# Two-layer FFN in half-size products: separate PSUM banks with vector sums, or shared PSUM banks with ScalarE copies of partial sums

## The chip, the cores and the metric

The kernel runs on one core of a Trainium2 chip. A core has five engines with a queue of instructions each, worked off strictly in the order of the queue: TensorE (PE; its weight loads are listed apart as PEld) for matrix products, VectorE (DVE), ScalarE (ACT) and GpSimd (POOL) for elementwise work, and SyncE (SP), which here issues most DMAs. An instruction that waits for a semaphore holds up everything behind it on its engine. The matrix engine writes its results into PSUM, eight banks of 512 float32 columns on 128 partitions; all other tiles are in SBUF.

The metric is the device time of a whole execution in microseconds, as a median of several. Beside it stands one profiled execution with a trace of every instruction.

## What is computed

Eight batches of 1024 rows of 256 numbers go through an attention block without learned projections and then through a two-layer FFN, both with adaptive layer norm and gates that come from a small vector per batch. All of it is float32.

```python
x = L0_attn_x                                    # (8, 1024, 256)
mod = (silu(L0_c) @ L0_wmod).reshape(8, 6, 1, -1)
sa, ca, ga, sb, cb, gb = (mod[:, n] for n in range(6))
ga, gb = gates pushed away from zero (at least 0.25 in size)
h = layernorm(x) * (1 + ca) + sa
scores = einsum('nsd,ntd->nst', h * w_lhs, h * w_rhs)
x = x + ga * einsum('nst,ntd->nsd', softmax(scores), h)
h = layernorm(x) * (1 + cb) + sb
y = relu(h @ W1 + b1) @ W2 + b2                  # 256 -> 1024 -> 256
out = x + gb * y
```

## The kernel before

A batch is cut into eight row tiles of 128 rows (`i` = 0 to 7), and its FFN into two groups of 512 rows (`g` = 0, 1). The main loop runs over batches `b` and tiles `i`. A step (b, i) computes the scores of the tile two ahead (`direct`, tile `psc`, L412), copies them to SBUF on ACT (L419), mirrors the symmetric part by a DVE transpose and two DMAs (`mirror`, L435, `move`, L306 and L309), turns the row maximum on PE (`max_turn`, tile `pm`, L468), subtracts it on DVE (L475), takes the exponent on ACT (`exponent`, L484; `weights` does both), and multiplies an earlier tile with the values (`product`, tile `po`, L501). Tiles 1 and 2, 3 and 4, 6 and 7 are multiplied in pairs, with seven half-size products in the place of eight (`pair_begin`, L549, tile `pp`; `pair_end`, L593, tiles `pq`, `pr`; their left-hand sums `left_sums` on POOL; `pair_out` on DVE).

Between these stands the FFN of the batch before (`fb = b - 1`): group 0 in steps 0 to 3, group 1 in steps 4 to 7. Both of its layers use the same scheme of seven half-size products with sums before and after. In the first layer a *pair* is chunk `c` and chunk `c + 4` of the eight chunks of 128 hidden units, over the two halves of the 512 rows (`lo`, `hi`, 256 columns). The products of a pair go to three PSUM banks `pa`, `pb`, `pc`; `pa` is copied to SBUF by ACT (`kept`, L747), and its first half is used again by the seventh product (`pair_last`). DVE forms the result `f` in five sums (`pair_sums` and L779), POOL adds the last term (L780), ACT applies the relu (`pair_relu`, L789 and L790), and POOL forms the four differences that the second layer needs (`pair_turn`, L799 to L802). Two pairs stand in each of the steps 0, 1, 4 and 5. The second layer runs in steps 2 and 3, and 6 and 7 (`y_first`, `y_second`, L806, tiles `ya`, `yb`, `yc`, `yd`), with seven sums on DVE and a scaling with the gate on ACT (`y_gate`, L857). The result is transposed on DVE (`y_turn`), sent through DRAM and back, and added to `x` on POOL (`y_add`, L880).

Steps also prepare the next batch: statistics on DVE (L241), 1/std on ACT (`prepare_rstd`, L247 and L248), the normalised rows `xg` on ACT (`prepare_norm`, L281, with a small shift `rs` from DVE, L277), their transpose on DVE and through DRAM (`prepare_blocks`, tiles `T_a` and `X_a`, L322), and from it the two sides of the score product on ACT (`prepare_turn_apart`, L342, tiles `rT`, `lT`). `spare` takes small POOL operations from a queue. The last batch's FFN stands after the loop, with a direct second layer (`second`, L916).

Every engine's order is the order in which the code calls these functions; `pin` holds the scheduler to it. PSUM is three pools: two banks for scores (tag `s`), two for transposes and maxima (tag `t`), four for everything else (tag `a`).

Of the kernel before, what the change touches and what calls it, by code (L numbers as in the profile page):

```python
# [17 lines left out]
P = 128  # L18
# [6 lines left out]
def adaln_block_kernel(  # L25
# [30 lines left out]
    ps_s = ctx.enter_context(tc.tile_pool(name="ps_s", bufs=2, space=PSUM))  # L56
    ps_t = ctx.enter_context(tc.tile_pool(name="ps_t", bufs=2, space=PSUM))
    ps_a = ctx.enter_context(tc.tile_pool(name="ps_a", bufs=4, space=PSUM))
    dram = ctx.enter_context(tc.tile_pool(name="dram", bufs=1, space=bass.MemoryType.DRAM))

# [79 lines left out]
    def warm(n):  # L140

        pw = ps_s.tile([P, HALF], F32, tag="s", name=f"pw_{n}")
        nc.tensor.matmul(pw[:, :n], lhsT=zeros[:, :P], rhs=zeros[:, :n], start=True, stop=True)
# [12 lines left out]
    pt_c = ps_t.tile([P, HALF], F32, tag="t", name="pt_c")  # L156
# [18 lines left out]
    def columns(src, at):  # L175
        n = src.shape[0]
        pv = ps_t.tile([P, HALF], F32, tag="t", name=f"pt_v{at}")
        nc.tensor.transpose(pv[:, :n], src, ident[:n, :n])
        nc.scalar.copy(cols[:, ds(at, n)], pv[:, :n])
# [9 lines left out]
    def mod_rows(part, parts):  # L189

        pm = ps_a.tile([P, HALF], F32, tag="a", name=f"pmr_{part}")
        w = parts * D
        for k in range(ND):
            nc.tensor.matmul(  # L194
                pm[:B, :w],
                lhsT=scT[:, k, :],
                rhs=wm[:, k, ds(part * D, w)],
                start=(k == 0),
                stop=(k == ND - 1),
            )  # L200
        nc.scalar.copy(
            mod[:, part : part + parts, :].rearrange("b s d -> b (s d)"), pm[:B, :w]
        )

    def mod_columns(part):

        pc = ps_a.tile([P, HALF], F32, tag="a", name=f"pmc_{part}")
# [140 lines left out]
    def prepare_turn(b, g, vector=True):  # L348
# [5 lines left out]
        for k in range(ND):  # L354
            if b > 0:
                pt = pre[b, g][:, k]
            else:
                pt = ps_t.tile([P, HALF], F32, tag="t", name=f"pth_{b}_{g}_{k}")
# [44 lines left out]
    def direct(b, i, parts=range(S // HALF)):  # L403
        if i == 0 and parts[0] == 0:
            sc_t[b] = two.tile([P, NT, NV, NT, V], F32, tag="sc", name=f"sc_{b}", bufs=1)
        for n in parts:
# [3 lines left out]
            psc = ps_s.tile([P, HALF], F32, tag="s", name=f"psc_{b}_{i}_{n}")  # L410
# [33 lines left out]
    def mirror_first(i):  # L444
        sc = first_scores()
        j = i + 1
        while j < NT:
            n = min(TH, NT - j)
            pool, tag = (ps_t, "t") if j == i + 1 else (ps_a, "a")
            pt = pool.tile([P, HALF], F32, tag=tag, name=f"ptm_{i}_{j}")  # L450
# [15 lines left out]
    def max_turn(b, i):  # L466
        pm = ps_t.tile([P, HALF], F32, tag="t", name=f"pm_{b}_{i}")
# [25 lines left out]
    def product(b, i, parts=(0, 1)):  # L493
        pT = pT_t[b, i]
        if 0 in parts:
            po_t[b, i] = ps_a.tile([P, HALF], F32, tag="a", name=f"po_{b}_{i}")
# [42 lines left out]
    def pair_begin(b, i, between=None):  # L539

        W = work.tile([P, 2, D + 4], F32, tag="W", name=f"W_{b}_{i}", bufs=1)
        pp = ps_a.tile([P, HALF], F32, tag="a", name=f"pp_{b}_{i}")
# [36 lines left out]
    def pair_end(b, i):  # L579
# [3 lines left out]
        pq = ps_a.tile([P, HALF], F32, tag="a", name=f"pq_{b}_{i}")  # L583
        pr = ps_a.tile([P, HALF], F32, tag="a", name=f"pr_{b}_{i}")
        for out, lhs, rhs in (
# [5 lines left out]
        ):  # L591
# [95 lines left out]
    def ffn_turn(b, g):  # L687
        hT = two.tile([P, ND, HALF], F32, tag="hT", name=f"hT_{b}_{g}", bufs=1)
        split = lambda T: T.rearrange("p (t a v) -> p t a v", a=NV, v=V)
        if (b, g) == (0, 0):  # L690
            xn, X = ffn.pop(("xn", g))[0], []
            for k in range(ND):
                pt = ps_t.tile([P, HALF], F32, tag="t", name=f"ptx_{b}_{g}_{k}")
# [29 lines left out]
    pairs = {}  # L723

    def mm(out, lhsT, rhs):
        nc.tensor.matmul(out, lhsT=lhsT, rhs=rhs, start=True, stop=True)  # L726

    def pair_products(b, g, c, between=None):
# [6 lines left out]
        n = ts(c, P)  # L735
        s1, a22 = (w1[:, k, ds((c + NH) * P, P)] for k in range(2))

        pool, tag = (ps_s, "s") if b == B - 1 else (ps_a, "a")
        pa = ps_a.tile([P, HALF], F32, tag="a", name=f"pa_{b}_{g}_{c}")
        pb = pool.tile([P, HALF], F32, tag=tag, name=f"pb_{b}_{g}_{c}")  # L740
        pc = ps_a.tile([P, HALF], F32, tag="a", name=f"pc_{b}_{g}_{c}")
        mm(pa[:, lo], w1[:, 0, n], hT[:, 0, lo])
        mm(pa[:, hi], s1, hs[:, 0])

        tag, bufs = ("s1", 1) if b == B - 1 and c % 3 == 2 else ("kept", 2)
        kept = work.tile([P, HALF], F32, tag=tag, name=f"kept_{b}_{g}_{c}", bufs=bufs)
        nc.scalar.copy(kept, pa)  # L747
        mm(pb[:, lo], w1s[:, 0, n], hs[:, 1])
        mm(pb[:, hi], w1s[:, 1, n], hs[:, 2])
        mm(pc[:, lo], w1[:, 1, n], hT[:, 1, lo])  # L750
        mm(pc[:, hi], a22, hT[:, 0, hi])
        if between:
            between()
        pairs[c] = pa, pb, pc, kept

    def pair_sums(b, g, c):
        pa, pb, pc, kept = pairs[c]
        f = ffn["f"]
        u = work.tile([P, H2], F32, tag="u", name=f"u_{b}_{g}_{c}", bufs=2)
        pairs[c] = pa, kept, u  # L760
        far = f[:, c + NH, hi]
        nc.vector.scalar_tensor_tensor(
            u, pb[:, lo], b1_col(c), kept[:, lo], ALU.add, ALU.add
        )
        nc.vector.scalar_tensor_tensor(  # L765
            far, pb[:, hi], b1_step[:, c : c + 1], u, ALU.add, ALU.add
        )
        nc.vector.scalar_tensor_tensor(
            f[:, c, lo], pc[:, lo], b1_col(c), kept[:, lo], ALU.add, ALU.add
        )  # L770
        nc.vector.tensor_tensor(f[:, c + NH, lo], pc[:, hi], far, ALU.add)

    def pair_last(b, g, c):


        pa, kept, u = pairs.pop(c)
        f = ffn["f"]
        mm(pa[:, lo], w1s[:, 2, ts(c, P)], ffn["hT", g][0][:, 1, hi])
        nc.vector.tensor_tensor(f[:, c, hi], pa[:, lo], u, ALU.add)  # L779
        nc.gpsimd.tensor_tensor(  # L780
            f[:, c::NH, hi],
            f[:, c::NH, hi],
            kept[:, None, hi].to_broadcast([P, 2, H2]),
            ALU.add,
        )

    def pair_relu(c):
        f = ffn["f"]
        nc.scalar.activation(f[:, c, :], f[:, c, :], AF.Relu)  # L789
        nc.scalar.activation(f[:, c + NH, :], f[:, c + NH, :], AF.Relu)  # L790

    def pair_turn(c):


        f, ft = ffn["f"], ffn["ft"]
        add = nc.gpsimd.tensor_tensor
        add(ft[:, 0, c], f[:, c + NH, hi], f[:, c, hi], ALU.subtract)  # L799
        add(ft[:, 1, c], ft[:, 0, c], f[:, c, lo], ALU.add)  # L800
        add(ft[:, 2, c], ft[:, 1, c], f[:, c + NH, lo], ALU.subtract)
        add(f[:, c, hi], f[:, c, hi], f[:, c, lo], ALU.subtract)  # L802

    def over_pairs(out, lhs, rhs):
        for c in range(NH):
            nc.tensor.matmul(  # L806
                out, lhsT=lhs(c), rhs=rhs(c), start=(c == 0), stop=(c == NH - 1)
            )

    def y_first(b, g, between=None):  # L810

        Y = ffn["Y"] = two.tile([P, 2, HALF], F32, tag="Y", name=f"Y_{b}_{g}", bufs=1)
        f, ft = ffn["f"], ffn["ft"]
        ya = ps_a.tile([P, HALF], F32, tag="a", name=f"ya_{b}_{g}")
        yb = ps_a.tile([P, HALF], F32, tag="a", name=f"yb_{b}_{g}")
        over_pairs(ya[:, lo], lambda c: w2[:, c, 0:P], lambda c: f[:, c, lo])
        over_pairs(yb[:, lo], lambda c: w2[:, c + NH, 0:P], lambda c: f[:, c + NH, lo])
        nc.scalar.copy(Y[:, 0, lo], ya[:, lo])
        if between:
            between()  # L820
        over_pairs(ya[:, hi], lambda c: w2s[:, 1, c], lambda c: ft[:, 1, c])
        over_pairs(yb[:, hi], lambda c: w2[:, c, P:D], lambda c: ft[:, 0, c])
        ffn["y"] = ya, yb

    def y_first_sums():
        Y, (ya, yb) = ffn["Y"], ffn.pop("y")
        add = nc.vector.tensor_tensor
        add(Y[:, 1, hi], ya[:, hi], Y[:, 0, lo], ALU.add)
        add(Y[:, 0, lo], yb[:, lo], Y[:, 0, lo], ALU.add)
        add(Y[:, 1, lo], yb[:, hi], Y[:, 1, hi], ALU.add)  # L830

    def y_second(b, g, between=None):

        f, ft = ffn["f"], ffn["ft"]
        yc = ps_a.tile([P, HALF], F32, tag="a", name=f"yc_{b}_{g}")
        yd = ps_a.tile([P, HALF], F32, tag="a", name=f"yd_{b}_{g}")
        over_pairs(yc[:, lo], lambda c: w2s[:, 0, c], lambda c: f[:, c, hi])
        if between:
            between()
        over_pairs(yc[:, hi], lambda c: w2s[:, 2, c], lambda c: f[:, c + NH, hi])  # L840
        over_pairs(yd[:, lo], lambda c: w2[:, c + NH, P:D], lambda c: ft[:, 2, c])
        ffn["y"] = yc, yd

    def y_second_sums(b):

        Y, (yc, yd) = ffn["Y"], ffn.pop("y")
        add = nc.vector.tensor_tensor
        add(Y[:, 0, hi], yc[:, lo], Y[:, 1, hi], ALU.add)
        add(Y[:, 1, hi], yc[:, lo], Y[:, 1, lo], ALU.add)
        add(Y[:, 0, hi], yc[:, hi], Y[:, 0, hi], ALU.add)  # L850
        add(Y[:, 1, lo], Y[:, 1, lo], yd[:, lo], ALU.subtract)

    def y_gate(b):

        Y = ffn["Y"]
        for h in range(2):
            nc.scalar.activation(  # L857
                Y[:, h], Y[:, h], AF.Identity,
# [593 lines left out]
```

## Time and profile before

| | us |
|---|---|
| two runs | 757.01, 758.22 (median 757.62) |
| profiled execution, first to last instruction | 755.1 |
| one batch in the middle (b = 3, at 258 to 349 us) | about 90.5 |
| busy DVE / ACT / POOL | 574.9 / 374.9 / 570.9 |
| granted TensorE clock | 1.000 |

Mean durations of what is added, removed or moved, from the groups of the page (form: output tile):

| line, engine, operation | ns | count |
|---|---|---|
| L747 ACT copy `kept<-pa` 128x512 | 584 | 64 |
| L789 ACT relu `f` 128x512 | 622 | 64 |
| L484 ACT exponent `pT` 128x1024 | 1056 | 64 |
| L818 ACT copy `Y<-ya` 128x256 | 384 | 14 |
| L762, L765, L768 DVE sum of three 128x256 | 475 to 484 | 64 each |
| L771, L779 DVE sum of two 128x256 | 414, 404 | 64 each |
| L780 POOL sum 128x512 | 1274 | 64 |
| L799 to L802 POOL difference 128x256 | 727 to 729 | 56 each |
| L475 DVE subtract 128x1024 | 1208 | 64 |

In a timeline row the first number is the start in us from the beginning of the span, the second the time from that start to the end of the last of the merged instructions. A matrix instruction in float32 appears as two records, each with a modelled end that overlaps the next start; the distance between starts is what TensorE takes. A bracket at a row's end tells how long the engine stood idle before it and which operation it then waited for.

### The profile page before, as it was taken

Reading aid. Unit: us, or ns where it says so; the run is one execution under the profiler, and the core shown is the slowest. Engines: PE = TensorE matmul, PEld = TensorE weight load, DVE = VectorE, ACT = ScalarE, POOL = GpSimd, SP = SyncE. Lnnn points to the kernel's source line nnn. Section 1 sums busy time; section 2 is a strip of 40 time slices with the busy share of each in tenths; the row PEclk is TensorE's granted clock in tenths of the full one; section 3 lists DMA queues with packets and bytes.
Section 4 is the critical chain, followed back from the end, with each engine's and each line's share of the span. In section 5 each row is a group of like instructions: output and inputs, shape, how many; then the busy total and the mean of one; then the engine's idle time right before and its main releaser. Section 6 shows DMA issues by size and latency. Waiting matters only on the chain.

```text
span 755.1 us, 11883 instructions
## 1 busy us (share of the span) xinstructions
PE 749.1 (99%) x3876; PEld 623.4 (83%) x3876; DVE 574.9 (76%) x1259; ACT 374.9 (50%) x688; POOL 570.9 (76%) x658
## 2 busy tenths in 40 slices
PE   8999999999999999999999999999999999999998
PEld 4686889788897888888888878988889788888887
DVE  7787879778796879968878688876889777685632
ACT  4554646635375454745546444563546535252521
POOL 3762796878968798788877699777996888669741
PEclk9999999999999999999999999999999999999999
DMA  9033442455443453445534555245553354133220
GB/s 308 16 112 98 131 133 74 135 178 152 127 120 123 153 153 110 147 118 158 164 99 119 153 154 161 74 127 172 155 152 85 119 166 133 50 91 126 84 85 28
DMA packets 106213, 95.21 MB, mean 126 GB/s; under 512 B 29700, under 2 KB 98848, under 8 KB 106152
## 3 DMA queue, kind: packets, MB, share of 16 engines
q1 hardware_dynamic: 98408, 85.81, 38.6%
q10 hardware_dynamic: 7744, 8.65, 3.7%
q8 instruction: 30, 0.49, 0.3%
q14 instruction: 31, 0.25, 0.1%
HBM read 50.62 MB, written 43.81 MB: 125 GB/s over the span
## 4 chain that ended last, share of the span: by engine, by line
PE 96%; DMA 1%; DVE 1%; ACT 1%; issue 0%
PE psc L412 16%; PE pa L726 11%; PE po L501 10%; PE pr L593 7%; PE pb L726 7%; PE pc L726 7%; PE yc L806 6%; PE ya L806 6%; PE yb L806 6%; PE pq L593 5%; PE pp L549 5%; PE py L916 4%; PE yd L806 3%; DMA wm<-in_L_wmod_dram 1%; PE pm L468 1%; PE pmr L194 0%
## 5 line engine op out<-in xcount | busy, mean ns | idle before, releaser
L412 PE MATMUL psc<-rT,lT 128*128 128x512 f32 (+3 forms) x384 | 134.8, 487 | 0.0
L780 POOL TENSOR_TENSOR f<-f,kept 128x512 f32<-128x512 f32 x64 | 81.5, 1274 | 42.8 <-DVE f L779 20.1
L419 ACT COPY sc<-psc 128x512 f32<-128x512 f32 (+3 forms) x96 | 44.7, 476 | 119.9 <-PE psc L412 113.0
L484 ACT ACTIVATE pT<-pT 128x1024 f32<-128x1024 f32 x64 | 67.6, 1056 | 70.6 <-DVE pT L475 70.5
L475 DVE TENSOR_TENSOR pT<-sc,pm 128x1024 f32<-128x1024 f32 x64 | 77.3, 1208 | 29.3 <-PE pm L468 13.7
L412 PEld LDWEIGHTS psc<-rT,lT 128*128 128x128 f32 x384 | 66.4, 191 | 37.2 <-issue 25.6
L501 PE MATMUL po<-xg,pT 128*128 128x257 f32 x352 | 80.6, 380 | 0.0
L463 DVE TENSOR_REDUCE m<-sc 128x1 f32<-128x1024 f32 x64 | 77.4, 1209 | 2.2 <-ACT sc L419 1.8
L501 PEld LDWEIGHTS po<-xg,pT 128*128 128x128 f32 x352 | 66.2, 190 | 10.0 <-issue 0.7
L747 ACT COPY kept<-pa 128x512 f32<-128x512 f32 x64 | 37.4, 584 | 69.3 <-PE pa L726 69.1
L726 PE MATMUL pb<-hs,w1s 128*128 128x256 f32 x256 | 65.9, 380 | 0.1
L726 PE MATMUL pc<-hT,w 128*128 128x256 f32 x256 | 65.7, 379 | 0.0
L880 POOL TENSOR_TENSOR x<-x,Y 128x512 f32<-128x512 f32 x28 | 35.1, 1276 | 29.3 <-DMA Y<-D_y 29.3
L789 ACT ACTIVATE f<-f 128x512 f32<-128x512 f32 x64 | 39.8, 622 | 34.7 <-POOL f L780 34.7
L642 POOL TENSOR_TENSOR x<-x,rows 128x256 f32<-128x256 f32 x64 | 44.8, 732 | 13.8 <-ACT rows L1022 10.6
L726 PEld LDWEIGHTS pb<-hs,w1s 128*128 128x128 f32 x256 | 48.5, 190 | 7.3 <-DVE f L765 0.8
L726 PEld LDWEIGHTS pc<-hT,w 128*128 128x128 f32 x256 | 48.6, 190 | 6.7
L806 PE MATMUL yc<-f,w2s 128*128 128x256 f32 x224 | 51.3, 379 | 0.0
L435 DVE STREAM_TRANSPOSE Tm<-sc 128x896 f32<-128x896 f32 (+6 forms) x49 | 34.3, 701 | 20.3 <-ACT sc L419 19.6
L806 PEld LDWEIGHTS yc<-f,w2s 128*128 128x128 f32 x224 | 41.5, 190 | 8.1 <-issue 2.9
L549 PEld LDWEIGHTS pp<-xg,pT 128*128 128x128 f32 x336 | 41.9, 192 | 5.1 <-DVE st_b L241 1.4
L799 POOL TENSOR_TENSOR ft<-f 128x256 f32<-128x256 f32 x56 | 40.8, 729 | 6.8 <-ACT f L790 6.8
(166 smaller groups left out, 1821.1 us busy)
## 6 DMA issues: line engine op xcount, KB each, us to landing
D_f<-T_f SPq DMA_DIRECT2D x60, 128.0 KB, 2.5
X_f<-D_f SPq DMA_DIRECT2D x15, 512.0 KB, 3.7
D_a<-T_a SPq DMA_DIRECT2D x56, 128.0 KB, 2.8
D_y<-T_y SPq DMA_DIRECT2D x56, 128.0 KB, 2.9
Y<-D_y SPq DMA_DIRECT2D x14, 512.0 KB, 3.4
out_dram<-x SPq DMA_DIRECT2D x14, 512.0 KB, 4.4
X_a<-D_a SPq DMA_DIRECT2D x13, 512.0 KB, 3.4
x<-in_L_attn_x_dram ACTq DMA_DIRECT2D x12, 512.0 KB, 3.4
```

Source lines behind the costliest of these rows:

```text
L412: nc.tensor.matmul(psc[:, : hi - lo], lhsT=lT_t[b, i // TH][:, k, ts(i % TH, P)], rhs=rT_t[b, n][:, k, lo - n * HALF : HALF], start=(k == ...
L419: nc.scalar.copy(score_row(b, i)[:, lo // V : hi // V, :], psc[:, : hi - lo].rearrange("p (n v) -> p n v", v=V),)
L463: nc.vector.tensor_reduce(m, score_row(b, i), AX.XY, ALU.max)
L475: nc.vector.tensor_tensor(pT.rearrange("p j (a v) -> p j a v", v=V), score_columns(b, i), pm[:, :P].rearrange("p (j a v) -> p j a v", j=1, ...
L484: nc.scalar.activation(pT_t[b, i], pT_t[b, i], AF.Exp)
L501: nc.tensor.matmul(po[:, : D + 1], lhsT=pT[:, t, :], rhs=xg_t[b][:, t, 0 : D + 1], start=(t == 0), stop=(t == NT - 1),)
L549: nc.tensor.matmul(out, lhsT=lhs[:, t, :], rhs=xg_t[b][:, h * TH + t, P : P + XS], start=(t == 0), stop=(t == TH - 1),)
L593: nc.tensor.matmul(out, lhsT=lhs[:, t, :], rhs=rhs[:, t, :], start=(t == 0), stop=(t == TH - 1),)
L642: queue.append(lambda: nc.gpsimd.tensor_tensor(out, in0, row, op))
L726: nc.tensor.matmul(out, lhsT=lhsT, rhs=rhs, start=True, stop=True)
L780: nc.gpsimd.tensor_tensor(f[:, c::NH, hi], f[:, c::NH, hi], kept[:, None, hi].to_broadcast([P, 2, H2]), ALU.add,)
L806: nc.tensor.matmul(out, lhsT=lhs(c), rhs=rhs(c), start=(c == 0), stop=(c == NH - 1))
```

## The change

The products of both layers are no longer kept in separate halves of banks and summed by DVE and POOL; they are added up in PSUM by the matrix engine, in two chains. Two chunks `c`, `c + 1` with their partners form a *unit*; a bank holds the same product for both. Bank A takes product one, then six, seven and four on top of it; bank E takes five and then three; bank B takes two. Between two additions ACT copies the partial sum to SBUF (`k1`, `k2`, `k5`), and DVE adds such a copy, the bias and the contents of another bank in one operation. The relu of the quarter that product four finishes is done by ACT straight from PSUM. The second layer does the same with `ya` in bank A (products one, six, seven, four) and `yc` in bank E (five, three). The number and shapes of the matrix products stay as they were.

PSUM becomes one pool with fixed banks: two for scores, one for maxima, A, B, E, and two (tag `o`) for `po`, `pp`, `pq`, `pr`. The steps are written anew (`step_units` for i = 0, 1, 4, 5, `step_rows` for the others, `tail` for the last batch). Attention products are put between the operations of a unit: `product` in steps 0 and 5, `pair_begin` in step 1, `pair_end` in step 4. Moved as well: `prepare_turn_apart(b + 1, 0, ...)` from step 4 to the end of step 3; `mirror` ahead of `y_turn` in step 4; `exponent` in step 4 stands in the queue of ACT ahead of the relus of `unit_four`; products of the second layer that were in step 2 go partly behind `pair_end`.

```diff
-    ps_s = ctx.enter_context(tc.tile_pool(name="ps_s", bufs=2, space=PSUM))
-    ps_t = ctx.enter_context(tc.tile_pool(name="ps_t", bufs=2, space=PSUM))
-    ps_a = ctx.enter_context(tc.tile_pool(name="ps_a", bufs=4, space=PSUM))
+    psum = ctx.enter_context(tc.tile_pool(name="psum", bufs=1, space=PSUM))
+    BANKS = {"s": 2, "m": 1, "A": 1, "B": 1, "E": 1, "o": 2}
...
+    def pair_mm(out, weights, c, rhs, first):
+        for q in range(2):
+            mm(
+                out[:, side[q]], weights(slice((c + q) * P, (c + q + 1) * P)), rhs,
+                first and q == 0,
+            )
+    def keep(tag, src, name):
+        k = work.tile([P, HALF], F32, tag=tag, name=name, bufs=1)
+        nc.scalar.copy(k, src)
+        return k
+    def unit_start(b, g, c, other=""):
...
+        A, E = bank(other or "A", f"pa_{at}"), bank(other or "E", f"pe_{at}")
+        pair_mm(A, lambda n: w1[:, 0, n], c, hT[:, 0, lo], True)
+        k1 = keep("k1", A, f"k1_{at}")
+        pair_mm(E, lambda n: w1[:, 0, far(n)], c, hs[:, 0], True)
+        k5 = keep("k5", E, f"k5_{at}")
+    def unit_two(c):
...
+        pair_mm(Bk, lambda n: w1[:, 1, n], c, hT[:, 1, lo], True)
+        for q in range(2):
+            nc.vector.scalar_tensor_tensor(
+                f[:, c + q, lo], Bk[:, side[q]], b1_col(c + q), k1[:, side[q]], ALU.add, ALU.add
+            )
+    def unit_six(c):
+        at, A, hs = unit[c][0], unit[c][1], unit[c][6]
+        pair_mm(A, lambda n: w1s[:, 0, n], c, hs[:, 1], False)
+        unit[c].append(keep("k2", A, f"k2_{at}"))
+    def unit_three(c):
...
+        pair_mm(E, lambda n: w1s[:, 2, n], c, hT[:, 1, hi], False)
+        for q in range(2):
+            nc.vector.scalar_tensor_tensor(
+                f[:, c + q, hi], E[:, side[q]], b1_col(c + q), k2[:, side[q]], ALU.add, ALU.add
+            )
+    def unit_seven(c):
...
+        pair_mm(A, lambda n: w1s[:, 1, n], c, hs[:, 2], False)
+        for q in range(2):
+            nc.vector.scalar_tensor_tensor(
+                f[:, c + q + NH, hi], A[:, side[q]], b1_col(c + q + NH), k5[:, side[q]],
+                ALU.add, ALU.add,
+            )
+    def unit_four(c, vector=False):
...
+        pair_mm(A, lambda n: w1[:, 1, far(n)], c, hT[:, 0, hi], False)
+        for q in range(2):
+            out, bias = f[:, c + q + NH, lo], b1_col(c + q + NH)
+            if vector:
+                nc.vector.tensor_scalar(out, A[:, side[q]], bias, 0.0, ALU.add, ALU.max)
+            else:
+                nc.scalar.activation(out, A[:, side[q]], AF.Relu, bias=bias)
...
+    def y_six():
+        Y, ft = ffn["Y"], ffn["ft"]
+        over_pairs(ffn["ya"][:, lo], lambda c: w2s[:, 1, c], lambda c: ft[:, 1, c], False)
+        nc.scalar.copy(Y[:, 0, hi], ffn["ya"][:, lo])
...
+    def step_units(b, i, ahead, late, extra):
...
+        unit_start(fb, fg, c)
+        if i == 0:
+            ffn_rstd(b - 1, 1)
+        elif i == 4:
+            y_gate(fb)
+            if more:
+                prepare_rstd(b + 1, 1)
+        if ahead:
+            mirror(*ahead)
+        unit_two(c)
+        if i == 4:
+            y_turn(fb, 0)
+        max_turn(*late)
+        unit_six(c)
...
+        if i != 4:
+            subtract(*late)
+        if extra:
+            exponent(*late)
+        unit_three(c)
...
+        elif i == 4 and more:
+            prepare_norm(b + 1, 1)
+            x_plus(b + 1, 1)
...
+        relu_left(c)
...
+        if i == 1:
+            pair_begin(b, i, lambda: unit_seven(c))
+        elif i == 4:
+            pair_end(b, 3, lambda: unit_seven(c))
+        else:
+            main(0)
...
+        relu_right(c)
+        turn_first(c)
...
+        if i == 4:
+            if more:
+                prepare_blocks(b + 1, 1)
+                xg_times(b + 1, 1)
+            weights(*late)
+        main(1)
+        unit_four(c)
+        if i == 1:
+            pair_begin_sum(b, i)
+        if ahead and ahead != extra:
+            row_max(*ahead)
...
+        if i in (0, 4):
+            turn_last(c)
...
+        if i == 3:
+            left_sums(b, i)
+            if more:
+                prepare_turn_apart(b + 1, 0, 1)
+                prepare_turn_apart(b + 1, 0, 0)
```

## The prediction

> **What bounds it now.** I read the page's busy times and chain first, then the waits of TensorE, then the timeline of one batch in the middle (258 to 349 us).
>
> ```profile
> span 755.1 us, 11883 instructions
> PE 749.1 (99%) x3876; PEld 623.4 (83%) x3876; DVE 574.9 (76%) x1259; ACT 374.9 (50%) x688; POOL 570.9 (76%) x658
> ...
> PE 96%; DMA 1%; DVE 1%; ACT 1%; issue 0%
> ```
>
> TensorE is busy for 749.1 of 755.1 us and is 96% of the chain. Its own waits are four:
>
> ```profile
> PE pw L143 <- DVE early_a L131: 1.5, 1, 1.5
> PE pmc L210 <- ACT cols L179: 0.5, 1, 0.5
> PE pmr L194 <- DMA wm<-in_L_wmod_dram: 0.4, 1, 0.4
> PE ya L806 <- ACT Y L818: 0.3, 1, 0.3
> ```
>
> Together 2.7 us. "Busy" could hide slow streaming, so I looked at when pieces start, at the end of step i = 4 and the start of step 5 (columns: start, duration, engine, line, tile, count):
>
> ```profile
> 306.67 1.06 PE L593 MATMUL pq<-tsum,pT 128*128 128x129 f32 x8
> 307.56 1.06 PE L593 MATMUL pr<-xg,pT 128*128 128x128 f32 x8
> 308.45 0.61 PE L412 MATMUL psc<-rT,lT 128*128 128x128 f32 x4
> 308.90 0.60 PE L726 MATMUL pa<-hT,w 128*128 128x256 f32 x2
> 309.34 0.59 PE L726 MATMUL pa<-hs,w 128*128 128x256 f32 x2
> ```
>
> Start to start: eight records of 128 columns take 0.89 us, two of 256 take 0.43, without a hole (durations overlap, so starts count). A half-size product (one matmul, two records) costs 0.43; a unit's operation (two of them) 0.86; a y block (four) 1.73. TensorE has nothing to win: only a new wait on it can move the time much, and every microsecond of such a wait is paid in full.
>
> **The change, part by part.** *TensorE.* Both programs list 2004 matrix instructions with 445,736 output columns, in the same shapes. Saved or added: 0.
>
> *Other engines.* Per unit (two chunk pairs) DVE drops from ten 128x256 sums (0.40 to 0.48 each) to six; POOL from two 1.27 us corrections and eight 0.73 differences to four of 1.27 (8.4 to 5.1 us). ACT gains a third copy (0.58) and reads the last product from PSUM itself. All of this is work beside TensorE: its loss gains nothing, at most the 2.7 us.
>
> *New waits, four per unit.* None can be below nothing, since there is no hole to close. All durations are those of the one profiled execution. Bank A takes product one, is copied (k1), takes six, is copied (k2), takes seven, is read by DVE, takes four, is read by two ACT relus, and only then is free for the next unit; E likewise takes five, k5, three. For each I put TensorE's next need against the copy. After the last matmul's successor starts, ACT was seen to begin 0.20 later (268.33 to 268.53) and DVE 0.27 (269.19 to 269.46). How long TensorE needs from the release to its first matmul is not shown alone; 0 is the lower end, the 0.35 us with which ya waited for Y at 686.71 the upper, and I take 0.1 to 0.15, as at 312.97, where a release by DVE delayed pb by 0.07 and the block after it by 0.11.
> - six after k1: product five and two lie between, 1.72 us, against 0.20+0.58. Covered, if ACT is free.
> - three after k5: product two, the max turn and six, 1.83. Covered.
> - seven after k2: three (0.86) plus half a product (1.73) or half of pair_begin (0.89). Covered; in step 4 by 2.6.
> - four after DVE's two sums on seven: 0.27+0.40+0.48+0.15 = 1.3. Steps 0 and 5 have 1.73 between, step 4 has 2.67, step 1 only the second half of pair_begin, 0.89. Wait 0.45 in each of 7 batches: **3.2 us**.
> - next unit after the relus: 0.20+0.33+0.38+0.1 = 1.0 at best (two operations of ACT overlap a little: relus of 0.61 start 0.52 apart; 0.38 from ACT's 128x256 PSUM copy L818; bounds 0.25, the 128x128 copy, and 0.61, the relu of 128x512). Steps 0, 1 and 5 have score products of 1.7 us and more between. Step 4 has only psc of 128 columns, 0.44.
>
> *Step 4 is where the order matters.* ACT's old queue there, one batch:
>
> ```profile
> 299.38 1.52 ACT L857 ACTIVATE Y<-Y,gcol 128x512 f32<-128x512 f32 x2
> ...
> 303.38 2.08 ACT L281 ACTIVATE xg<-x,rs,ra 128x256 f32<-128x256 f32 x4 [0.76 <-DVE rs L277]
> 305.36 0.61 ACT L789 ACTIVATE f<-f 128x512 f32<-128x512 f32 x1
> 305.88 0.61 ACT L790 ACTIVATE f<-f 128x512 f32<-128x512 f32 x1
> 306.39 1.50 ACT L342 ACTIVATE rT<-X_a,sides 128x512 f32<-128x512 f32 x2
> 307.81 1.51 ACT L342 ACTIVATE lT<-X_a,sides 128x512 f32<-128x512 f32 x2
> 309.22 1.04 ACT L484 ACTIVATE pT<-pT 128x1024 f32<-128x1024 f32 x1
> ```
>
> The four rT/lT operations (2.9 us) move to the end of step 3. Their X_a, issued at 293.13 and landing 4.15 later as at 313.87, is there at 297.28, so they hold ACT until 299.9, while step 4's first product starts at 297.84. Behind them stand the score copy (to 300.2), k1 (300.75), k5 (301.25), the gates of 256 and 512 columns (302.5), the two rstd operations (302.95) and k2 (303.5). Six is wanted at 297.84+2.69 = 300.53 and starts at 300.95: wait 0.4. From there TensorE: six to 301.8, three 302.7, s1 and a22 304.45, seven 305.3, the rest of pair_end 307.98, four 308.84, psc 309.28.
>
> DVE: y_turn waits for the gates, 302.55 to 303.8; three's sums behind it and k2, to 304.6; rs to 304.9; then ACT's norms 304.95 to 307.0 and the relus; T_a on DVE 307.05 to 308.3; subtract to 309.46 (1.18); exponent 309.5 to 310.55 on ACT. The two relus that free A are queued behind that exponent: done at 311.15, first matmul about 311.35, wanted at 309.28. Wait 2.1. Step 4 costs 2.5 per batch, in the six batches with a successor (b = 1 to 6): **15.0 us**. In b = 7 norms and rT/lT are missing and the floor 1.0-0.44 remains: 0.6.
>
> *One of a kind.* In (b, i) = (1, 0) the product now follows the exponent at once: pm read at +3.0, subtract 1.2 behind two sums, exponent 1.06: ready at about +6.2, wanted at +5.5: 0.7. In the tail the second half of a row tile meets fresh relus: 0.3 twice, 0.6.
>
> *Moved, and covered.* y_turn is now behind mirror on DVE and SP: four writes of Y (1.8 us of SP) after the 2.4 of the score mirror; X_a's read goes ahead of Y's. T_a ends 1.5 later, but SP issued D_a only at 308.89, so X_a still lands near 318; rT, the relus, lT and four's relus then end near 323.5, and y_one wants bank A at about 325.5. Cover 2.0; without it 2.0 x 6. POOL's y_add waits for Y with two turns behind it, needed near 330: it has some 4 us. In the y blocks each copy of ya (0.2+0.38) has a whole block of 1.73 over it; without, the 0.35 seen, x14 = 4.9. One bank for pm, and two for po/pp/pq/pr in place of four: pair_out ends reading pq near 290 when pp wants it at 290.3. Thin, taken as 0, upper end 0.4 x 7.
>
> Sum: 15.0+3.2+0.6+0.7+0.6 = 20.1. Span 755.1+20.1 = 775.2. The median of the runs, 757.6, is 2.5 above the span: **777 us**, +2.6%.
>
> **Two rules weighed.** Cold matrix records are in the page's groups:
>
> ```profile
> L412 PE MATMUL psc<-rT,lT 128*128 128x512 f32 x192 | 89.3, 593 | 0.0
> L143 PE MATMUL pw<-early_a 128*128 128x512 f32 x4 | 4.1, 1141 | 1.5 <-DVE early_a L131 1.5
> ```
>
> The same shape takes 1141 ns at the start and 593 later; the granted clock is 1.00 in every stretch. With gaps of 2.1 us I keep the warm rate. The Trainium skill, "TensorE: Matmul & The Clock Gate", Part 1, says the clock halves after an idle window of about 3.4 us; were the gaps that long, about 3.4 us at half rate after each would make an estimated 1.7 x 6 = 10 more, 787.
>
> Four's relus could go to DVE, whose sum from PSUM takes 0.48 against ACT's 0.38; DVE is done with subtract at 309.46, so bank A would be free near 310.4 and the wait 1.2, 5 us less in all. The skill's "ScalarE: Activation LUTs", Rules for kernel authors, speaks for that and against this change: it puts relu on VectorE; by it the sum would be 772.
>
> **Rivals.** (1) *Not slower: step 4's ACT queue runs as early as it did.* Before, norms began 5.5 us after the first product; I have 7.1. If they begin by 5.5, exponent and relus end 1.6 earlier and only the floor is left: 7 x 0.6+3.2+1.3 = 8.7, 766. For it: overlapping ACT operations and an earlier mirror in step 1, which may pull X_a forward. Against it: k1 to k2 are in one queue behind rT/lT. It decides at a step 4 cost of 1.6.
> (2) *Every new wait also loses the preloaded weights.* 0.18 as at 312.97, for four waits in 32 units and four in 14 y groups: 184 x 0.1 to 0.18 = 18 to 33, 795 to 810. Against it: the old pair_last waited for kept 64 times with no row of waiting.
> (3) *Freed engines help TensorE*: at most its 2.7 us: 755.
> (4) *The change not doing what it says*: the lists show it, PE equal, DVE 1215 to 1031, POOL 656 to 479, ACT 707 to 781.
>
> **Numbers.** Forecast 0.62 (own range 770 to 786), rival 1 0.28 (760 to 772), rival 2 0.08, rival 3 0.02. A run tells about 2% from no change, 742.5 to 772.8. Faster 0.01; same: rival 1, rival 3 and the lower edge of the forecast, 0.33; slower 0.66. Range 761 to 790.
>
> **What would show it.** In the waits: PE pa <- ACT f (the PSUM relu), about 2 us, six times, and PE pa <- DVE f, 0.45, seven times; ACT's exponent ahead of the two PSUM relus, ending after psc has run out. PE near 749 busy in a span near 775, DVE and POOL lower. Wrong, if norms start within 5.6 us of step 4's first product, or the waits lie in the y blocks.

## The result, and the profile after

| | before | after |
|---|---|---|
| median of the runs, us | 757.62 | 781.02 (780.81, 781.24) |
| profiled span, us | 755.1 | 779.0 |
| granted TensorE clock | 1.000 | 1.000 |

After stands to before as 1.0307 (95% interval 1.0277 to 1.0336): slower, 4 us above the forecast and inside its range. First the page's head and its chain of waits:

```profile
span 779.0 us, 11552 instructions
PE 757.4 (97%) x3876; PEld 624.4 (80%) x3876; DVE 506.5 (65%) x1075; ACT 409.0 (52%) x762; POOL 473.7 (61%) x481
...
PE 76%; ACT 11%; DVE 6%; issue 5%; DMA 1%; DVEq 0%
```

DVE lost 68 us of work and POOL 97, and the span grew by 23.9. TensorE, 96% of the chain before, is 76% now: ACT and DVE have become links. TensorE's waits (total, times, longest):

```profile
PE pa L738 <- ACT f L817: 9.9, 7, 1.6
PE ya L738 <- ACT Y L855: 2.1, 6, 0.7
PE pw L152 <- DVE early_a L140: 1.4, 1, 1.4
PE ya L738 <- ACT f L817: 1.1, 1, 1.1
PE yc L738 <- DVE Y L877: 0.9, 1, 0.9
PE pmc L219 <- DVE x L523: 0.8, 1, 0.8
PE pmc L219 <- ACT cols L188: 0.5, 1, 0.5
PE pm L476 <- DVE pT L483: 0.3, 1, 0.3
PE py L954 <- ACT f L817: 0.2, 1, 0.2
```

The wait rows understate the loss, because a record's modelled end runs past the next start, and DVE's sums on product seven (0.24 us each time) have no row at all. So I counted *holes*: the distance between two starts on TensorE, less the median distance that this shape has in the trace. Taking what is above 0.05 us, before has 5.6 us of holes and after 29.2; the difference, 23.7, is the difference of the spans (23.9) to within 0.2. Behind almost every hole the block's next record comes 0.1 us late as well; the sums below include it.

| hole (times) | forecast, us | found, us |
|---|---|---|
| step 5's first product, bank A from step 4 (6) | 12.6 | 11.1 |
| step 4's six after k1 (6) | 2.4 | 1.5 |
| the same bank A at b = 7 | 0.6 | 0.75 |
| step 1's four after the sums on seven (7) | 3.2 | 2.4 |
| (1, 0): second max turn and product | 0.7 | 0.7 |
| tail | 0.6 | 0.9 |
| second layer's six after the copy of Y (6) | 0 | 3.75 |
| b = 7: y_one, y_three | 0 | 2.5 |
| head: pmc | 0 | 1.0 |
| sum | 20.1 | 24.6 |

Some 0.8 us of small holes behind the first 20 us are not in the table, and before has 1.6 us there of its own; 24.6 + 0.8 - 1.6 is the 23.8 that the two kernels differ by in that part.

Step 4 of a middle batch, in the timeline (start, duration, engine, line, tile, count, idle before and its releaser):

```profile
312.63 2.08 ACT L290 ACTIVATE xg<-x,rs,ra 128x256 f32<-128x256 f32 x4 [1.35 <-issue]
...
314.74 1.30 DVE L331 STREAM_TRANSPOSE T_a<-xg 128x512 f32<-128x512 f32 x2 [0.37 <-ACT xg L290]
...
315.97 1.18 DVE L483 TENSOR_TENSOR pT<-sc,pm 128x1024 f32<-128x1024 f32 x1
...
316.83 0.61 PE L421 MATMUL psc<-rT,lT 128*128 128x128 f32 x4
...
317.18 1.06 ACT L492 ACTIVATE pT<-pT 128x1024 f32<-128x1024 f32 x1 [1.01 <-DVE pT L483]
318.15 0.82 ACT L817 ACTIVATE f<-pa,cols 128x256 f32<-128x256 f32 x2
...
319.02 1.13 PE L738 MATMUL pa<-hT,w 128*128 128x256 f32 x4 [1.58 <-ACT f L817]
```

Read it as a relay. ACT's norms (312.63) let DVE transpose T_a (314.74); only then does DVE subtract (315.97). ACT idles 1.01 us for that subtract with the exponent at the head of its queue, and the two relus that free bank A stand behind the exponent. Product four, which they read, was issued at 315.97: its result lay waiting. TensorE had four records of psc left, 0.44 us from 316.83, so it wanted bank A at 317.27 and got it at 319.02.

The miss is in step 6:

```profile
332.18 0.27 PE L476 MATMUL pm<-ident,m 128*128 128x128 f32 x1
332.29 1.89 PE L738 MATMUL ya<-f,w 128*128 128x256 f32 x8
332.56 1.22 DVE L483 TENSOR_TENSOR pT<-sc,pm 128x1024 f32<-128x1024 f32 x1 [0.82 <-PE pm L476]
333.86 1.07 ACT L428 COPY sc<-psc 128x512 f32<-128x512 f32 x2 [3.77 <-issue]
334.02 1.89 PE L738 MATMUL yb<-f,w 128*128 128x256 f32 x8
334.81 1.07 ACT L492 ACTIVATE pT<-pT 128x1024 f32<-128x1024 f32 x1
...
335.77 0.38 ACT L855 COPY Y<-ya 128x256 f32<-128x256 f32 x1
...
336.20 2.00 PE L738 MATMUL ya<-ft,w2s 128*128 128x256 f32 x8 [0.30 <-ACT Y L855]
```

The first block ended near 334.0, and its copy could have begun there. But ACT had stood for 3.77 us at the score copy: it starts 0.08 after the subtract's end, and that subtract reads `sc`, of which there is one buffer (the row names no releaser, so this link is read from the times and the tile names). Behind it came the exponent, and only then the copy of `ya`.

### The profile page after: what moved, and what is told of

Read it like the earlier page. It is cut to its first block, busy times and chain, and to the rows that moved or that the text cites. A ratio compares the mean times of both kernels' runs of the same rounds, so it can differ in the third digit from the quotient of the medians.

```text
span 779.0 us, 11552 instructions
## 1 busy us (share of the span) xinstructions
PE 757.4 (97%) x3876; PEld 624.4 (80%) x3876; DVE 506.5 (65%) x1075; ACT 409.0 (52%) x762; POOL 473.7 (61%) x481
## 4 chain that ended last, share of the span: by engine, by line
PE 76%; ACT 11%; DVE 6%; issue 5%; DMA 1%; DVEq 0%
PE psc L421 13%; PE pa L738 12%; PE ya L738 10%; PE po L509 9%; PE pe L738 6%; PE pr L603 5%; PE yc L738 5%; PE pp L557 4%; PE py L954 4%; PE pq L603 3%; PE pb L738 3%; ACT pT L492 2%; DVE pT L483 2%; PE yb L738 2%; ACT xg L290 2%
## 5 line engine op out<-in xcount | busy, mean ns | idle before, releaser
L836 POOL TENSOR_TENSOR ft<-f 128x512 f32<-128x512 f32 x28 | 35.7, 1274 | 74.4 <-ACT f L825 74.4
L738 PE MATMUL pa<-hT,w 128*128 128x256 f32 x256 | 67.5, 386 | 10.5 <-ACT f L817 9.9
L738 PEld LDWEIGHTS pa<-hT,w 128*128 128x128 f32 x256 | 46.8, 190 | 25.3 <-ACT f L817 13.4
L738 PE MATMUL pa<-hs,w1s 128*128 128x256 f32 x256 | 66.3, 381 | 0.1
L756 ACT COPY k<-pa 128x512 f32<-128x512 f32 x64 | 37.3, 583 | 47.7 <-PE pa L738 47.1
L803 DVE SCALAR_TENSOR_TENSOR f<-pa,cols,k 128x256 f32<-128x256 f32 x64 | 28.0, 480 | 38.9 <-PE pa L738 38.9
L738 PE MATMUL ya<-ft,w 128*128 128x256 f32 x224 | 52.9, 380 | 0.0
L738 PEld LDWEIGHTS pa<-hs,w1s 128*128 128x128 f32 x256 | 45.4, 191 | 8.1 <-POOL pT L584 2.0
L573 POOL TENSOR_TENSOR s<-pT 128x512 f32<-128x512 f32 x21 | 26.7, 1273 | 40.9 <-ACT pT L492 36.5
L724 POOL TENSOR_TENSOR hs<-hT 128x256 f32<-128x256 f32 x16 | 11.6, 725 | 60.5 <-DVE hT L715 60.5
```

What stands on the lines that cost most here:

```text
L738: nc.tensor.matmul(out, lhsT=lhsT, rhs=rhs, start=first, stop=True, skip_group_check=True)
L756: nc.scalar.copy(k, src)
L836: add(ft[:, 0, c : c + 2], f22, f12, ALU.subtract)
```

## The experiments

Theory 1: the loss is made of waits, each a bank released late by an in-order queue and wanted early by TensorE; moving the release ahead, or the use back, recovers it. Theory 2: adding up in one bank costs by itself. Theory 3: the fixed bank is the cost. (Where the expectations for step 4 speak of unit c = 2, the unit in step 4 is c = 0; c = 2 is that of step 5, which wants the bank.) All times below are medians beside the kernel before on the same chip; "span" is the profiled one, against 779.0 for the change.

**Step 4: the two relus ahead of the exponent.**

```diff
         if i == 4:
...
-            weights(*late)
         main(1)
         unit_four(c)
+        if i == 4:
+            weights(*late)
```

> Step 4 only: unit c=2's fourth product and its two ScalarE relus are put ahead of the weights (subtract and exponent) of the pair, so that the relus stand before the exponent in ScalarE's queue. Nothing is left out. Theory 1 (the time comes from the order of the queues: the bank of unit c=2 is wanted while ScalarE still has the exponent, which waits for VectorE's subtract, ahead of the relus): the hole of 1.85 us before the first score product of step 5 shrinks to about 0.75 (the exponent's 1.0 us and its idle go) six times, that is -6.6 us: span near 772.4 instead of 779.0. Theory 2 (adding up in a shared bank costs by itself: a later product into the same bank is slower or waits for its own predecessors, in whatever order): no change, 779 +- 0.5. Theory 3 (the fixed bank A is the cost, as the next block wants that very bank): the same hole remains, only with another name, at most -1.

Measured: 774.12 us, ratio 1.0219 (1.0203 to 1.0234), span 772.9. The six holes fell from 1.74 to 0.65 us each. That is theory 1's number to within half a microsecond; theories 2 and 3 in their pure form fall, since neither the adding up nor the banks changed.

**Step 4: product four one block earlier.**

```diff
-            if between and n == 2:
-                between()
+            if between and n in (2, 4):
+                between(n)
...
-            pair_end(b, 3, lambda: unit_seven(c))
+            pair_end(b, 3, lambda n: unit_seven(c) if n == 2 else unit_four(c))
```

> Step 4 only: unit c=2's fourth product is moved before the last product block of the pair's end (its relus so stand some 1 us earlier, and one more block of TensorE's work lies between it and the next use of its bank). Nothing is left out. Theory 1 (order of the queues): the hole of 1.85 us before step 5's first score product closes, six times: -11 to -12 us at b = 0 to 5 with b = 7's 0.75: span near 767.5. If the fourth product now waits for VectorE's sums of the seventh, up to 0.35 x 7 comes back (span up to 770). Theory 2 (adding up in a shared bank costs by itself): no change, 779 +- 0.5. Theory 3 (the fixed bank): no change or -1.

Measured: 772.02 us, ratio 1.0187 (1.0170 to 1.0204), span 771.0. All seven holes ahead of step 5 are gone, as expected, but the span is 3.5 above theory 1's. What came back is nearly all in b = 7, among TensorE's waits:

```profile
PE ya L738 <- ACT f L817: 2.9, 1, 2.9
```

and in ACT's and DVE's timeline there:

```profile
684.94 0.85 DVE L780 SCALAR_TENSOR_TENSOR f<-pb,cols,k 128x256 f32<-128x256 f32 x2
685.71 1.21 DVE L483 TENSOR_TENSOR pT<-sc,pm 128x1024 f32<-128x1024 f32 x1
686.84 0.87 DVE L794 SCALAR_TENSOR_TENSOR f<-pe,cols,k 128x256 f32<-128x256 f32 x2
687.63 1.03 DVE L665 SCALAR_TENSOR_TENSOR rs_f<-mvb,rb 128x4 f32<-128x4 f32 x1
...
688.69 2.08 ACT L668 ACTIVATE X_f<-x,rs_f,rb 128x256 f32<-128x256 f32 x4 [3.11 <-DVE rs_f L665]
```

and on POOL beside them:

```profile
687.36 1.28 POOL L844 TENSOR_TENSOR f<-f 128x512 f32<-128x512 f32 x1
```

TensorE reaches step 5 earlier, DVE does not: the tiny `rs_f` (four columns) stands behind a subtract and four sums, ACT's norms wait 3.11 us for it, and the exponent and the relus, the last two of which free bank A for `y_one`, wait behind the norms. `rs_f` itself took 1.03 us here and 0.15 at this place in the change: it starts within a POOL operation and ends 0.02 us after that one's end (688.64), as do 77 of the 86 cases over 0.3 us of this operation in all the traces. That hole grew from 1.3 to 3.1 us, and the records after it ran at half rate (below), 1.7 more: together the 3.5.

**Step 6: the copy of Y ahead of the exponent.**

```diff
                 max_turn(*late)
-                weights(*late)
+                subtract(*late)
                 y_one(fb, fg)
+                exponent(*late)
```

> Step 6 only: the exponent is recorded behind the first block of the second layer, so that ScalarE's copy of that block's partial sum stands ahead of it; the subtract keeps its place. Nothing is left out. Theory 1 (order of the queues): the sixth block's 0.56 us holes (five, and one of 0.93) go: -3.7 us, span near 775.3; the exponent 1.1 us later has the rest of the second layer's blocks over it. Theory 2 (adding up in the shared bank costs by itself): no change, 779 +- 0.5. If the exponent turns out to be on the path, a new hole before the values' product takes the place of the old one, and the span stays or rises.

Measured: 777.40 us, ratio 1.0261 (1.0245 to 1.0276), span 775.7. The six holes are gone, and no new hole came behind them.

**Step 4: the two relus on VectorE.**

```diff
-        unit_four(c)
+        unit_four(c, i == 4)
```

> Step 4 only: unit c=2's two relus from the bank go to VectorE (add the bias, then the maximum with 0) instead of ScalarE. Nothing is left out. Theory 1 (order of the queues): VectorE is free of the subtract at 317.15 where the relus on ScalarE began at 318.15, so the bank comes free some 0.9 us earlier: the hole of 1.85 shrinks to about 1.0, six times: -5 to -5.6 us, span near 773.6. Theory 2 (adding up in the shared bank costs by itself): no change. Theory 3 (the fixed bank): no change or -1. VectorE's own relus, if they cost more than 0.41 us each, give part of it back.

Measured: 778.37 us, ratio 1.0271 (1.0253 to 1.0288), span 776.7. At the place itself theory 1 holds: 1.74 became 0.71 us, six times, 6.2 in all. But 0.86 us more of DVE in each step 4 made `rs_f` late at b = 7 again (hole 3.1 us and a stretch at half rate, 3.5 in all over the change), so only 2.3 of it reached the span. A miss in the total, by the same b = 7 mechanism as above.

**The turn of lT and rT back in step 4.**

```diff
             left_sums(b, i)
-            if more:
-                prepare_turn_apart(b + 1, 0, 1)
-                prepare_turn_apart(b + 1, 0, 0)
...
         relu_left(c)
+        if i == 4 and more:
+            prepare_turn_apart(b + 1, 0, 1)
+            prepare_turn_apart(b + 1, 0, 0)
```

> The pair of ScalarE/GpSimd operations that turn the next batch's first half (ScalarE's 1.41 us operation ahead of step 4's first copy) go back from the end of step 3 into step 4, behind the left relu, where the kernel before had them. Nothing is left out. Theory 1 (order of the queues): the 0.25 us hole of the sixth product goes (-1.5 over six batches), but the 1.41 us stand again ahead of the exponent and the two relus that release unit c=2's bank; ScalarE had 1.01 us of idle ahead of the exponent, so 0.4 to 1.4 us are added to the hole of 1.85, six times: +2.4 to +8.5; net +1 to +7, span 780 to 786. If the move was what costs (a theory of the reordering as such), the span falls instead, to 775 or less.

Measured (one run): 797.56 us, span 795.8. Slower as expected, but by 16.8 us, more than twice the most expected. The holes grew from 1.74 to 2.98 us (one 3.26), +7.7, and k1's 1.5 went: that much was expected. Most of the rest, some 9.5 us, is TensorE's clock: after five of these six holes a stretch of records came at half rate. It is a control for the order theory (adding work ahead of the exponent lengthens the hole), and a warning on its size.

**Step 1: product seven half a block earlier.**

```diff
-            pair_begin(b, i, lambda: unit_seven(c))
+            pair_begin(b, i, None, lambda: unit_seven(c))
...
+                if early and h == 0 and t == 1:
+                    early()
```

> Step 1 only: unit c=2's seventh product is issued after the first half of the first product block of the pair's beginning instead of after the block's second, so that VectorE's two sums are done when the fourth product wants the bank. Nothing is left out. Theory 1 (order of the queues): the 0.345 us hole before step 1's fourth product goes, seven times: -2.4, span near 776.6. If VectorE is late because of other work in its queue and not for the seventh product's place, the hole stays and the span with it (779).

Measured (one run): 778.64 us, span 776.9; the seven holes are gone, as theory 1 has it.

**No adding up in the first layer.** The edit gives products three, four, six and seven `first = True`, so that they overwrite the partial sums, which this kernel leaves out (one of the four places is shown):

```diff
-        pair_mm(A, lambda n: w1s[:, 0, n], c, hs[:, 1], False)
+        pair_mm(A, lambda n: w1s[:, 0, n], c, hs[:, 1], True)
```

> The third, fourth, sixth and seventh products of every unit start their bank anew instead of adding to what stands in it: the partial sums of the first layer are left out, every instruction, its order, its operands and its waits stay. Theory 1 (only waits cost): no change, span 779 +- 0.7, the same holes at the same places. Theory 2 (adding up in a shared bank costs TensorE time by itself, in the writing or in the order of writes): the span falls; 23.9 us at most.

Measured (one run): 780.35 us, span 778.5, with 1.74 us at the same six places. Theory 2 falls for the first layer: writing on top of a partial sum cost TensorE 0.5 us of 779 at most. The second layer still adds up here; the last kernel below bears on it.

**The kernel before with less work on POOL.** The edit removes the call at L780, so one of the first layer's sums is left out.

> The kernel before without the 64 corrections on GpSimd (one of the first layer's sums is left out: the kept partial product is not added). This is the largest single relief that the change gives to an engine other than TensorE, without the change's new waits. Theory: TensorE is the bound at 99% and GpSimd is covered, so nothing: span 755.1 +- 0.7. Rival (freed engines help TensorE): 750 or less.

Measured (one run): 756.47 us beside 757.75 for the kernel before, span 754.5 against 755.1; that 0.6 us is in the holes of the first 60 us, where before waits 0.4 for a DMA and this run does not. Taking 78 us off POOL is worth nothing inside the loop. The change's relief of DVE was not tried alone; that it gains nothing either rests on the holes of before, which are 1.6 us in all behind the first 20 us.

**Step 5: banks A and B exchanged, nothing reordered.**

```diff
...
-        unit_start(fb, fg, c)
+        unit_start(fb, fg, c, "B" if i == 5 else "")
...
-        unit_two(c)
+        unit_two(c, "A" if i == 5 else "B")
```

> Step 5 only: unit c=2's first product takes the bank that its second had, and the second the bank that the first had. Queues and their order, instructions and counts stay; nothing is left out. The bank that ScalarE's two late relus of step 4 release is then wanted some 2.5 us later, and y_one's bank in step 6 was last read by VectorE's sums of the second product, not by the four relus. Theory 1, order of the queues with the fixed bank as its other half (a wait needs a late release and an early use): 1.85 x 6 + 0.75 in step 5 and 1.38 ahead of y_one at b = 7 go: -13, span near 766. Theory 2 (ScalarE as such is too slow for the new copies, and whatever bank is used, TensorE waits for it): the hole only moves to another product of step 5, span 775 or more. The sixth block's holes in step 6 (3.7), step 1's (2.4) and the rest stay.

Measured: 769.23 us, ratio 1.0152 (1.0134 to 1.0169), span 768.5. It is the best single edit: two calls, and two functions that take the bank's name. Of the 13 us 10.5 arrived: all eight holes closed, but 0.1 us stayed at each of six second products, new holes came in the second layer at b = 7 (1.1), and the head took 0.6 more. So the bank is the other half of the same wait: a late release costs only if the next use of that bank is early. The expectation's own theory 2, that TensorE would wait for ACT with any bank, falls with it (775 or more).

**All moves of order at once.** Beside the edits on product four, on the copy of Y and on product seven above:

```diff
         elif i == 4:
+            if more:
+                prepare_turn_apart(b + 1, 0, 0)
             y_gate(fb)
...
         unit_six(c)
+        if (b, i) == (B - 1, 5):
+            ffn_rstd(b, 0)
+            middle(b, i)
...
         if ending:
             pair_end(b, i - 1)
-            pair_out(b, i - 1)
-            pair_stats(b, i - 1)
...
             if ending:
+                pair_out(b, i - 1)
+                pair_stats(b, i - 1)
                 ffn_rstd(b, 1)
...
             unit_four(2)
+            begin(tiles[3])
...
-        pc = any_bank(f"pmc_{part}")
+        if part:
+            turn.rotate(-1)
+            pc = bank(turn[-2], f"pmc_{part}")
+        else:
+            pc = any_bank(f"pmc_{part}")
```

> All moves of order together, each at a place where the changed kernel's TensorE waits: step 4's fourth product ahead of the pair's last block; step 6's copy of Y ahead of the exponent; step 1's seventh product half a block earlier; ScalarE's turn of lT behind step 4's first copies; at b = 7 the norms of step 5 ahead of the third product and step 7's pair output behind y_five; in the last part the fourth tile's first half behind the fourth product; in the head another bank for the modulation columns. Nothing is left out. Theory 1 (all 23.9 us are waits of this order): 779.0 less 11.8, 3.7, 2.4, 1.5, 1.4, 1.2, 0.9 and 1.0 is 755.1, with 0.5 to 2 us of holes left: span 755.5 to 757.5, a time within 0.5% of the kernel before (757.6). The scheme of shared banks as a cost of its own: a remainder of 5 us or more, span 760 or above. TensorE's products being the same in number, no theory gives less than 754.

Measured: 762.39 us, ratio 1.0070 (1.0055 to 1.0085), span 760.6. By its number it stands on the other theory's side (760 or above). The waits say why that is no support for it: the first product of the tail waited for ACT's gate on `ya`, which I had put behind a square root that waits for DVE's statistics, a new hole of 2.2 us of my own making. Six of 0.2 ahead of step 5 and 1.1 ahead of `y_one` at b = 7 also remained. The last kernel below, without them, tells the theories apart.

**The same moves with the exchanged banks in place of the earlier product four.** The edit is the two pieces together, without the one on product four.

> As the kernel with all moves of order, but step 4's fourth product stays where the change has it, and instead step 5's first and second product exchange their banks. Nothing is left out. Theory 1: the same 755.5 to 757.5; where the fourth product ahead of the last block makes VectorE's or ScalarE's queue later at b = 7, this one does not, and is the shorter by up to 1 us. The scheme as a cost of its own: 760 or above.

Measured: 767.85 us, ratio 1.0137 (1.0120 to 1.0154), span 766.8: some 10 us above theory 1 and, by its number, on the other side again; the holes account for the 10. The lT turn, 1.4 us of ACT now in step 4, pushed the relus past even the later use of the bank: six holes of 0.97 us ahead of the second product, 6.4 in all with the record after. Without it, in the exchange alone, only the 0.1 was left there. The rest is the tail's hole (2.2, again mine) and 1.7 of half rate behind it.

**Both, with the square root moved.** Beside the two pieces:

```diff
             if ending:
                 pair_out(b, i - 1)
                 pair_stats(b, i - 1)
-                ffn_rstd(b, 1)
...
             y_four(fb)
+            if ending:
+                ffn_rstd(b, 1)
```

> The kernel with all moves of order, with the exchange of step 5's two banks added, and at b = 7 step 7's square root behind the fourth block of the second layer (before it, ScalarE waited for VectorE's statistics with that block's copy behind it, and the last part's first product waited 2.1 us for the bank). Nothing is left out. Theory 1: of that kernel's span of 760.6 the hole of 2.19 goes, six of 0.20 ahead of step 5, and 1.10 ahead of y_one at b = 7: 756.1, and a time within 0.5% of the kernel before. The scheme of shared banks as a cost of its own, beyond waits: 758.5 or more.

Measured: 758.52 us, ratio 1.0014 (1.0005 to 1.0023), span 756.6. The page's head and TensorE's waits:

```profile
span 756.6 us, 11551 instructions
PE 749.1 (99%) x3876; PEld 623.1 (82%) x3876; DVE 507.3 (67%) x1075; ACT 409.2 (54%) x762; POOL 474.4 (63%) x481
```

```profile
PE pw L152 <- DVE early_a L140: 1.5, 1, 1.5
PE pmc L223 <- ACT cols L188: 0.8, 2, 0.5
PE pmr L203 <- DMA wm<-in_L_wmod_dram: 0.6, 1, 0.6
PE pe L744 <- DVE Y L893: 0.4, 1, 0.4
PE pm L480 <- DVE pT L487: 0.3, 1, 0.3
```

Of the waits that the change put into its batches only the one in (1, 0) is left (`pm`; `pe` is in the tail); TensorE is busy for 749.1 us again, as before the change, to the tenth, and 22.4 of the 23.9 us are back. The other theory's 758.5 was meant for the span, as the 756.1 beside it was; the span is 0.5 above the one and 1.9 below the other. (That the median of the runs is 758.52 is chance: it stands 1.9 above the span.) Behind the first 20 us this kernel has 2.3 us of holes and before has 1.6, and the end behind TensorE's last start is 0.5 longer; little is left that a cost of adding up by itself, in either layer, could be. This is the change's own arithmetic with every product, copy and relu in it. It is still 1.1 us slower than the kernel before; no version here beats that one.

## Why the prediction was right

*What bounds it.* Right. With TensorE's products unchanged, freed engines gained nothing (POOL's 78 us: 0.6, in the first 60 us), and a wait on TensorE was paid in full: holes account for 23.7 of the 23.9.

*Step 4.* The mechanism was right link by link: norms, T_a, subtract, exponent, then the relus. The two edits that cut the chain in different places closed the hole. Sizes: 1.85 us (with the record after) against 2.1, because the norms began 6.7 us after the unit's first product and not 7.1; six after k1 0.25 against 0.4. Of 15.0, 12.6 came. The sum takes 0.2 from release to first product in step 4 (311.15 to 311.35), where its text says 0.1 to 0.15. Both were high: bank A's relus ended at 318.97 and the product began at 319.02.

*Step 1, (1, 0), tail, b = 7's floor.* 4.7 found, 5.1 forecast. Step 1's 0.45 was 0.345. In (1, 0) 0.54 of the 0.7 stands at the second max turn, which waited for the subtract to release the one bank of `pm`, and 0.17 at the product; the product waited for the exponent in either case (81.63, product at 81.68), so the chain is the forecast one.

*Luck in the number.* The terms that the prediction named came to 17.3 us for its 20.1, and 7.25 came from places that it had priced at 0; the two errors offset each other in part. Its own sum, 775.2 and 2.5 more, is 777.7, put down as 777; the runs stand 2.0 above the span, not 2.5.

*The step that failed*, in a prediction that was right on the whole, is "each copy of ya has a whole block of 1.73 over it", priced at 0. True of the product, not of the queue: it assumed that ACT was free, where in step 6 the score copies waited for DVE's subtract and the exponent came next. Found: 3.75 us. I had followed ACT's queue in step 4 but not in step 6; the upper end that I kept, 4.9, held it. With b = 7's 2.5 the second layer's blocks have 6.25 of the 24.6 us, and waits there were among the prediction's own signs of being wrong. "Cover 2.0" for `y_one` held in six batches and failed at b = 7, where `rs_f` is late (1.4). Beyond (1, 0), one bank for `pm` and two for `po` to `pr` cost nothing in the loop, as taken; in the head the bank of `pmc` cost 1.0, not foreseen.

*The rivals.* (1) falls: the norms did not start within 5.5 us. (2) falls, in its form: waits that were satisfied in time show no hole; only a late one costs 0.1 more at the next record. (3) falls for POOL by the kernel with less POOL work. (4) was never seen.

*The rules weighed.* On the clock: the row's side was right for the change. Holes of 1.74 us left the granted clock at 1.00. The 10 us that the Trainium skill's rule would have made of gaps of 3.4 us did not appear in the change, whose gaps are too short for that rule; an experiment lost 9.5 in this way, as told in the last section. On relu: the skill's "ScalarE: Activation LUTs", Rules for kernel authors, puts it on VectorE, and 5 us less was estimated; at that place 6.2 came, of which 2.3 reached the span. And the gain is not VectorE's speed: the pair took 0.86 us there against ACT's 0.82. It came from leaving a queue in which the exponent stood ahead.

## What to carry to other kernels

Where one engine is the bound and its work stays the same, taking load off the others gains nothing, and every value that it must now wait for has to be checked in the *queue* that delivers it, not by the distance between producer and consumer alone. A bank that is added to several times is held from its first product to its last reader: look for the step with the least work between that reader and the next use, and there either move the reader ahead of what waits, or give the next use another bank. Fixes of this kind move the wait; two of the three combined versions here had holes that I had made myself, which only their profiles showed.

## What the runs showed of the hardware

*The clock can fall after holes of two to three microseconds.* In the kernel with product four one block earlier, TensorE's stretches around b = 7's `y_one` (window, length, busy time and count of PE, PEld, DVE, ACT, POOL, then the granted clock):

```profile
694.30:697.40 3.10, 3.10 (x8) 2.47 (x8) 0.17 (x1) 1.06 (x1) 2.94 (x4) 0.51 0.49 116
697.40:700.00 2.60, 2.60 (x13) 2.29 (x13) 0.42 (x1) 0.37 (x1) 2.52 (x3) 1.00 0.93 294
```

After a hole of 3.1 us the granted clock is 0.51 for about 3 us, and the 256-column records start 0.43 us apart in place of 0.215. In all the runs: no such stretch after the holes of 1.74 us, nor after one of 2.08; one after a hole of 2.23; after five of six between 2.98 and 3.26, with the turn back in step 4; after both of 3.13. Seven of these eight stretches cost 1.5 to 1.7 us each, beyond the 0.1 that every hole costs; the eighth, after the hole of 3.26, ran at half rate for some 5.5 us and cost 2.9. The first record that they made late started 0.6 to 1.8 us after TensorE had resumed. The Trainium skill, "TensorE: Matmul & The Clock Gate", Part 1, speaks of a free-running window of about 3.4 us that must be idle; the varying start fits a window that runs by itself, and the estimate of 1.7 per stretch that I drew from it fits seven of the eight. That a hole of 2.23 us can suffice, seen once, does not fit an idle window of 3.4, and one hole of 2.98 brought no stretch; here the measurement decides: what two microseconds of waiting cost may nearly double with little more.

*A late product costs its neighbour too.* The record after a hole came 0.08 to 0.1 us late nearly every time, which is some 2.8 us of the loss over the batches.
